# A fused two-layer block on Trainium2: the order of work in its last stage is rearranged, and some copies move to other engines and to DMA

## The chip, the cores and the metric

The program runs on one core of one Trainium2 chip. The metric is device time in microseconds (us) for one execution, as the median of several runs. One further execution was recorded by the hardware profiler; all single durations come from that record.

## The reference

Sixteen sequences of 256 rows with 256 features go through four residual steps: cross-attention to a context of 77 rows, a mixture of experts, a second cross-attention with a mask and a factor per pair, and a gated linear attention with experts. Only the last step is touched. Cut to its core, it is:

```
q1, k1, v = x @ Wq * scale, x @ Wk, x @ Wv            # 8 heads of 64
q2 = x @ Wqa @ Wqb * scale                            # low-rank path
k2 = softmax(x @ Wka @ Wkb)                           # per head
gk1 = log_sigmoid(x @ Wg1a @ Wg1b + bg1) / 16         # decay of the dense path
gk2 = log_sigmoid(x @ Wg2a @ Wg2b + bg2) / 16         # decay of the routed path
e   = softmax(x @ We)                                 # 4 experts, the best one is kept
o   = gla(q1, k1, v, gk1) + sum over experts of gla(q2*e, k2*e, v, gk2*mask)
g   = x @ Wga @ Wgb
o   = o * rsqrt(mean(o*o over a head)) * norm_w * g * sigmoid(g)
x   = x + tanh(gate) * (o @ Wo)
```

Here x is normalised over its features first. `gla` is causal linear attention with a decay per feature, kept per chunk of 64 rows in the reference.

## The kernel before

The fast path does the first steps batch by batch and the last step in `stage3_fast` (L1619). There the 16 batches are cut into slots: slot p = 4b + m works on batch b and on the pair of heads m (128 of the 512 features). `for p in range(last)` at L2056 emits the slots one by one. Every operation of an engine in this stage is tied to program order, so the text of the loop is the order of each engine's queue; the engines wait for each other by semaphores. Nearly all vector, scalar and GpSimd operations are recorded under L50 (a wrapper), the matmuls under L1637 and the transposes on TensorE under L1640.

What a slot does, with the names that the profile shows as tiles:

- `masked(p - 1, 1)` (L1917): VectorE multiplies the second product of the slot before with shares and mask, from PSUM into `at1`; GpSimd adds it to `at0` (profile: `at<-at,at`).
- `keys_queries(p + 1)` (L1834): TensorE, keys and queries of the next slot into the PSUM bank `kq`.
- `decays(p + 1)` (L1842): cumulative decays by TensorE into `gq` and `gz`, then four exponentials `ee` on ScalarE.
- `products(p, 0)` and `products(p, 1)` (L1903): query-key products of the dense and the routed path into `sc`, a pair of banks of which there is only one (pool `psa`).
- `masked(p, 0)`: VectorE, mask of the first product.
- `factors(p + 1)` and `factors_second(p + 1)` (L1888, L1895): VectorE and GpSimd multiply keys and queries with the exponentials, tiles `f`, `q`, `k`.
- `second(p + 1)` (L1854): low-rank queries into `gq`, low-rank keys of a batch ahead into `gz`.
- `summed(p)` (L2051): `values(p - 1)`, matmuls of `at` with `v` into the bank `o`, and on even p the squares of the result on ScalarE.

Around this, tables name the steps for a batch that run once in four slots. Each entry is a step, how many batches ahead it works, and perhaps an index; `run` looks up slot p % 4. They are `start` (ahead of `masked`), `copies` (behind it), `middle` (behind `keys_queries`), `rest` (ahead of `decays`), `late` (behind it), `behind_mask`, `by_rows` (behind `factors`) and `logs` (behind `factors_second`, ahead of `products(p, 1)`):

```
start = {2: [(turn_hot, 1)]}
copies = {2: [(turned_hot, 1)]}
middle = {0: [(lows, 1)], 1: [(all_gates, 1)], 2: [(pairs, 1)], 3: [(scaled, 0, 0)]}
rest = {0: [(bias, 2)], 1: [(route, 1)], 2: [(steepest, 1, 0), (stats, 2)], 3: [(steepest, 1, 1), (turn_ahead, 2)]}
late = {1: [(scaled, -1, 1)], 2: [(project, -1)], 3: [(vals, 1)]}
logs = {0: [(route_sums, 1), (outgates_end, 0, 0)], 1: [(outgates_end, 0, 1), (gate_logs, 1, 0)], 2: [(gate_logs, 1, 1), (norm_ahead, 2)]}
```

The steps: `stats`, `norm_ahead` and `turn_ahead` take the mean and variance of a batch's rows (VectorE, then four small operations on GpSimd, `rs`), normalise (ScalarE, `xn`) and transpose (`xnT`) two batches ahead. `lows` (L1689) makes the low-rank rows `low`, with the copy `lowd` by DMA and the copy `low2` on VectorE. `route_logits`, `route_sums` and `route` choose the expert (tiles `e`, `eden`, `eq`, `hot`); `turn_hot`, `turned_hot` and `pairs` turn the choice into masks (`em`, `am`). `all_gates` (L1754) makes the decays' logits in two banks and in the pair of banks `sc`. `outgates` (L1807) makes the output gate: matmuls `zg`, exponential `eg`, copy `zs`; `outgates_end` ends it with `gw` on GpSimd. `shares` and `shares_end` give the softmax's sums. `gated`, `scaled` and `project` finish a batch (`u`, `r`, `oT`, `proj`). Single banks of PSUM come from a pool of two in rotation (`pss`), others (`kq`, `gq`, `gz`, `o`) exist once.

All along, `check` collects maxima and sums; at the end `Verdict` looks at them, and if a bound was passed the program runs a slower path. `check["second"]` holds the largest sums of the second softmax.

Of the kernel before, what the change touches and what calls it, by code (L numbers as in the profile page):

```python
# [10 lines left out]
F32 = mybir.dt.float32  # L11
I32 = mybir.dt.int32
AF = mybir.ActivationFunctionType
ALU = mybir.AluOpType
AX = mybir.AxisListType
PSUM = bass.MemoryType.PSUM

P = 128
B, S, D = 16, 256, 256
# [4 lines left out]
V_LN1G, V_LN1B, V_LN2G, V_LN2B, V_QB, V_KB, V_NW, V_ONE, V_GATE, V_N = 0, 2, 4, 6, 8, 10, 12, 13, 14, 18  # L24
# [49 lines left out]
def layers(ctx: ExitStack, tc: tile.TileContext, t, out, check):  # L74
    nc = tc.nc
# [6 lines left out]
    def const(name, shape, dtype=F32):  # L82
        return cp.tile(list(shape), dtype, tag=name, name=name)


    xs, cs = [None] * B, [None] * B
# [42 lines left out]
    vec = const("vec", [P, V_N])  # L129
# [47 lines left out]
    dve3, act3, pool3 = free = [Pinned(tc, x, False) for x in (nc.vector, nc.scalar, nc.gpsimd)]  # L177
# [41 lines left out]
    def normed(dst, src, mv, rs, p=P, n=2):  # L219
        for i in range(n):  # L220
            act.activation(dst[:, i, :], src[:, i, :], AF.Identity, bias=rs[:p, 1, i:i + 1],
                           scale=rs[:p, 0, i:i + 1])

    def turned_squares(xT, x, portion):

        for n in portion:
            q, r = n // 4 * 32, n % 4 * 32
            dve.transpose(xT[r:r + 32].rearrange("p k (i s) -> p i k s", i=2)[:, :, :, q:q + 32],
                          x[q:q + 32].rearrange("p i (k d) -> p i k d", k=2)[:, :, :, r:r + 32])
# [319 lines left out]
    if fast:  # L549
        route = Route()  # L550
# [1068 lines left out]
    def stage3_fast(early_bank):  # L1619

        with ExitStack() as sx:
# [3 lines left out]
            def of(b):  # L1625

                return w1 if b % 2 else w0

            def bank(name):
                return pss.tile([P, 512], F32, tag="ps", name=name) if pss else early_bank(name)  # L1630
# [5 lines left out]
            def matmul(*a, **k):  # L1636
                tc.keep_in_program_order(nc.tensor.matmul(*a, **k))  # L1637
# [10 lines left out]
            low2 = w1.tile([64, P], F32, tag="low2", name="low2")  # L1648
# [4 lines left out]
            xn, xnT, low, lg, hT, em, am, lowd = {}, {}, {}, {}, {}, {}, {}, {}  # L1653
            v, gw, u_, oT = {}, {}, {}, {}


            mvs = {}
# [13 lines left out]

            def norm_ahead(b):
                xn[b] = w0.tile([P, 2, D], F32, tag="xn", name="xn")
                normed(xn[b], xs[b], *mvs.pop(b))

            def turn(b):
                xnT[b] = of(b).tile([P, 2, S], F32, tag="xnT", name="xnT")
# [6 lines left out]
            def turn_ahead(b):  # L1684

                xnT[b] = of(b).tile([P, 2, S], F32, tag="xnT", name="xnT")
                turned_squares(xnT[b], xn[b], range(16))

            def lows(b):  # L1689

                low[b] = of(b).tile([P, 2, S], F32, tag="low", name="low")
                ps = bank("low")
                for c in range(2):
                    for k in range(2):
                        matmul(ps[:, c * S:(c + 1) * S], la[:, k, c * P:(c + 1) * P], xnT[b][:, k, :],
                                         start=k == 0, stop=k == 1)
                dve3.tensor_copy(low[b][:, 0, :], ps[:, :S])
                dve3.tensor_scalar(low[b][:, 1, :], ps[:, S:], vec[:, V_ONE:V_ONE + 1], None, ALU.add)
                lowd[b] = of(b).tile([P, S], F32, tag="lowd", name="lowd")
                nc.sync.dma_start(out=lowd[b][64:], in_=low[b][:64, 1, :])  # L1700
                if b > 0:
                    for r in range(0, 64, 32):
                        dve3.tensor_scalar(low2[r:r + 32, :], ps[64 + r:96 + r, S + P:],
                                           vec[64 + r:96 + r, V_ONE:V_ONE + 1], None, ALU.add)

            e_, den_, z_ = {}, {}, {}

# [99 lines left out]
            def outgates(b):  # L1807

                gw[b] = w2.tile([P, 4, S], F32, tag="gw", name="gw")
                two = [bank("zg"), bank("zg")]  # L1810
                for i in range(2):
                    for h, (w, x) in enumerate(((lbg[0:64], low[b][0:64, 1, :]), (lbg2[64:], lowd[b][64:]))):
                        m = 2 * i + h
                        matmul(two[h][:, i * S:(i + 1) * S], w[:, m * P:(m + 1) * P], x, start=True, stop=True)
                for h, ps in enumerate(two):
                    e, zs = (w2.tile([P, 512], F32, tag=n, name=n) for n in ("eg", "zs"))
                    act3.activation(e, ps, AF.Exp, scale=-1.0)
                    act3.copy(zs, ps)
                    z_[b, h] = zs, e

            def outgates_end(b, h):
# [55 lines left out]
            def shares_end(b):  # L1877
                ps = z_.pop((b, "den"))
                den = w2.tile([P, 8, 32], F32, tag="dens", name="dens")
                dve3.transpose(den.rearrange("p x j -> p (x j)"), ps[:, :S])  # L1880
                rd[b] = st.tile([P, 8, 2], F32, tag="kden", name="kden")
                flat = rd[b].rearrange("p x j -> p (x j)")
                most = check["second"].rearrange("p (x j) -> p x j", j=2)
                dve3.tensor_tensor(most, most, den[:, :, 0::16], ALU.max)
                dve3.reciprocal(rd[b], den[:, :, 0::16])
                pool3.tensor_tensor(check["rsum"][:, :16], check["rsum"][:, :16], flat, ALU.add)

# [62 lines left out]
            def squares(b, mp):  # L1950
                if mp == 0:
                    u_[b] = w2.tile([P, 4, S], F32, tag="u", name="u")
                    oT[b] = w2.tile([P, 4, S], F32, tag="oT", name="oT")
                ps = o.pop((b, mp))
                sq[b, mp] = w2.tile([P, 512], F32, tag="sq", name="sq")
                act3.activation(sq[b, mp], ps, AF.Square)
                z_[b, mp, "o"] = ps
# [45 lines left out]
                    matmul(ps, ones, v[B - 1][:, 0, :], start=True, stop=True)  # L2003


            start = {2: [(turn_hot, 1)]}
            copies = {2: [(turned_hot, 1)]}
            middle = {0: [(lows, 1)], 1: [(all_gates, 1)], 2: [(pairs, 1)], 3: [(scaled, 0, 0)]}

            rest = {0: [(bias, 2)], 1: [(route, 1)], 2: [(steepest, 1, 0), (stats, 2)], 3: [(steepest, 1, 1), (turn_ahead, 2)]}  # L2010
            late = {1: [(scaled, -1, 1)], 2: [(project, -1)], 3: [(vals, 1)]}
            behind_mask = {0: [(route_logits, 1)]}
            by_rows = {0: [(outgates, 0)], 1: [(gates_end, 1)]}
            logs = {0: [(route_sums, 1), (outgates_end, 0, 0)], 1: [(outgates_end, 0, 1), (gate_logs, 1, 0)], 2: [(gate_logs, 1, 1), (norm_ahead, 2)]}

            def run(steps, p):
                for f, d, *a in steps.get(p % 4, ()):
                    if 0 <= p // 4 + d < B:
                        f(p // 4 + d, *a)
# [16 lines left out]
            w1 = sx.enter_context(tc.tile_pool(name="f3w1", bufs=1, reuse_waits="tile"))  # L2036
            w2 = sx.enter_context(tc.tile_pool(name="f3w2", bufs=2, reuse_waits="tile"))
            psa = sx.enter_context(tc.tile_pool(name="f3psa", bufs=1, space=PSUM, reuse_waits="tile"))
            pss = sx.enter_context(tc.tile_pool(name="f3ps", bufs=2, space=PSUM, reuse_waits="tile"))
            last = 4 * B  # L2040
            decays(0)
            for m in range(0, 3, 2):
                ps = bank("k2")
# [7 lines left out]
            def summed(p):  # L2051
                values(p - 1)
                if p % 2 == 0:
                    squares((p - 1) // 4, (p - 1) % 4 // 2)

            for p in range(last):  # L2056
                if p == 0:
                    turn(1)
                run(start, p)
                if p % 4 == 0:  # L2060
                    shares(p // 4)
                if 0 < p:
                    masked(p - 1, 1)
                run(copies, p)
                if p % 4 == 0:
                    shares_end(p // 4)
                if 1 < p and p % 2 == 1:
                    gated((p - 2) // 4, (p - 2) % 4 // 2)
                if p + 1 < last:
                    keys_queries(p + 1)  # L2070
                run(middle, p)
                run(rest, p)
                if p + 1 < last:
                    decays(p + 1)
                run(late, p)
                products(p, 0)
                masked(p, 0)
                run(behind_mask, p)
                if p + 1 < last:
                    factors(p + 1)  # L2080
                run(by_rows, p)

                inside = p % 4 > 0 and p + 1 < last
                if inside:
                    summed(p)
                if p + 1 < last:
                    second(p + 1)
                    factors_second(p + 1)
                run(logs, p)
                products(p, 1)  # L2090
                if 0 < p and not inside:
                    summed(p)

            b, p = B - 1, last - 1
# [126 lines left out]
```

## Time and profile before

| what | value |
|---|---|
| median of 3 runs | 1845.09 us (1840.51 to 1845.21) |
| profiled execution, its own time | 1847.08 us |
| span of the profiled execution | 1845.3 us |
| last stage, one batch in its steady part | 37.72 us |
| TensorE busy over the span | 1813.5 us (98%) |
| VectorE, ScalarE, GpSimd busy | 1231.5, 873.9, 1017.0 us |
| granted TensorE clock, mean | 0.995 |

The span runs from the first to the last instruction of the program in the profiled execution. The names in a row are the tile written, an arrow, and the tiles read; then the shapes, the number of instructions and, in brackets, the idle time before and what ended it. PE stands for TensorE, PEld for its weight loads, DVE for VectorE, ACT for ScalarE, POOL for GpSimd and SPq for the queue that issues DMAs. A matmul's end is modelled in such a record, so distances between starts are the better measure of TensorE's pace. A row in a timeline that holds several instructions gives the time from the first start to the last end.

### The profile page before, as it was taken

Reading aid. Unit: us, or ns where it says so; the run is one execution under the profiler, and the core shown is the slowest. Engines: PE = TensorE matmul, PEld = TensorE weight load, DVE = VectorE, ACT = ScalarE, POOL = GpSimd, SP = SyncE. Lnnn points to the kernel's source line nnn. Section 1 sums busy time; section 2 is a strip of 40 time slices with the busy share of each in tenths; the row PEclk is TensorE's granted clock in tenths of the full one; section 3 lists DMA queues with packets and bytes.
Section 4 is the critical chain, followed back from the end, with each engine's and each line's share of the span. In section 5 each row is a group of like instructions: output and inputs, shape, how many; then the busy total and the mean of one; then the engine's idle time right before and its main releaser. Section 6 shows DMA issues by size and latency. Waiting matters only on the chain.

```text
span 1845.3 us, 35182 instructions
## 1 busy us (share of the span) xinstructions
PE 1813.5 (98%) x13870; PEld 1249.8 (68%) x13870; DVE 1231.5 (67%) x2903; ACT 873.9 (47%) x1804; POOL 1017.0 (55%) x1001
## 2 busy tenths in 40 slices
PE   8999999999999999999999999999999999999997
PEld 5666666666766667666777766656767777777765
DVE  3355656566665666656474488867888878878874
ACT  4433344433444334443433487846555645455543
POOL 4654767567676576756634767315444444444433
PEclk9999999999999999999999999999999999999999
DMA  9800010000010100000077933100000000000000
GB/s 304 226 1 22 16 34 15 25 17 23 23 37 8 29 19 10 31 23 18 13 248 238 233 49 49 18 4 3 14 8 10 8 10 13 8 9 8 14 9 14
DMA packets 68504, 85.86 MB, mean 47 GB/s; under 512 B 10740, under 2 KB 55908, under 8 KB 67818
## 3 DMA queue, kind: packets, MB, share of 16 engines
q1 hardware_dynamic: 56041, 66.74, 11.5%
q0 software_dynamic: 12288, 16.79, 4.5%
q8 instruction: 111, 1.82, 0.4%
q14 instruction: 64, 0.52, 0.1%
HBM read 44.17 MB, written 38.29 MB: 45 GB/s over the span
## 4 chain that ended last, share of the span: by engine, by line
PE 82%; POOL 9%; DVE 4%; issue 2%; ACT 2%; DMA 1%; SPq 0%; POOLq 0%; DVEq 0%; ACTq 0%
PE o L50 11%; PE qk L50 11%; PE v L50 8%; PE sc L50 8%; PE proj L50 7%; PE kq L1637 7%; PE sc L1637 5%; POOL es L50 4%; PE gq L1637 3%; PE v L1637 3%; PE o L1637 3%; PE proj L1637 3%; POOL x L50 2%; PE ex L50 2%; POOL rs L50 2%
## 5 line engine op out<-in xcount | busy, mean ns | idle before, releaser
L50 POOL TENSOR_SCALAR rs<-mv 128x2 f32<-128x2 f32 (+2 forms) x85 | 16.3, 192 | 376.8 <-DVE mv L50 371.1
L50 DVE RECIPROCAL rd<-o 128x256 f32<-128x256 f32 x64 | 112.3, 1755 | 164.0 <-PE o L50 123.7
L50 POOL TENSOR_TENSOR at<-at,at 128x768 f32<-128x768 f32 x63 | 114.1, 1812 | 142.4 <-DVE at L50 142.4
L50 ACT ACTIVATE e<-sc 128x1024 f32<-128x1024 f32 (+1 forms) x192 | 181.7, 1016 | 18.4 <-PE sc L50 18.4
L50 PE MATMUL sc<-qk 64*128 64x256 f32 (+1 forms) x1536 | 183.1, 384 | 0.5 <-DVE qk L50 0.5
L50 PE MATMUL o<-e,v 128*32 128x256 f32 (+1 forms) x3072 | 177.9, 379 | 0.0
L50 PEld LDWEIGHTS sc<-qk 64*128 64x128 f32 (+1 forms) x1536 | 132.0, 172 | 55.1 <-issue 26.8
L50 POOL TENSOR_TENSOR esum<-esum,es 128x512 f32<-128x512 f32 x128 | 163.5, 1277 | 10.0
L50 PE MATMUL qk<-kvT,wkv 128*128 128x333 f32 x512 | 164.3, 443 | 0.0
L50 ACT ACTIVATE qk<-qk 128x256 f32<-128x256 f32 x128 | 48.8, 381 | 231.4 <-PE qk L50 231.4
L50 POOL TENSOR_TENSOR es<-e 128x1024 f32<-128x1024 f32 x64 | 151.2, 2363 | 12.1 <-ACT e L50 9.0
L50 POOL TENSOR_TENSOR es<-es,e 77x1024 f32<-77x1024 f32 x64 | 150.4, 2350 | 5.0
L50 PEld LDWEIGHTS o<-e,v 128*32 128x32 f32 (+1 forms) x3072 | 99.9, 110 | 66.3
L50 PE MATMUL qk<-kvT,wq 128*128 128x256 f32 x512 | 134.6, 385 | 0.0
L50 DVE COPY qk<-qk 128x333 f32<-128x333 f32 x128 | 64.6, 504 | 93.8 <-ACT qk L50 92.8
L50 POOL DMA_INDIRECT x<-rows_out,pos x64 | 101.1, 1580 | 33.2 <-issue 17.0
L50 PEld LDWEIGHTS qk<-kvT,wq 128*128 128x128 f32 x512 | 94.3, 189 | 35.2 <-issue 9.6
L50 PEld LDWEIGHTS qk<-kvT,wkv 128*128 128x128 f32 x512 | 97.2, 190 | 30.0
L50 PE MATMUL proj<-wo0h,oT 128*128 128x256 f32 x512 | 113.7, 380 | 0.3 <-DVE oT L50 0.3
L50 PE MATMUL v<-wkv,kvT 128*128 128x512 f32 x256 | 113.1, 595 | 0.0
L50 PEld LDWEIGHTS proj<-wo0h,oT 128*128 128x128 f32 x512 | 95.9, 190 | 13.9 <-issue 0.8
L50 POOL DMA_INDIRECT rows<-xw,pos x64 | 66.8, 1043 | 61.1 <-ACT xT L50 24.0
(265 smaller groups left out, 4085.7 us busy)
## 6 DMA issues: line engine op xcount, KB each, us to landing
rows<-zero SPq DMA_DIRECT2D x16, 640.0 KB
xin<-rows SPq DMA_DIRECT2D x16, 640.0 KB
rows_out<-y SPq DMA_DIRECT2D x16, 384.0 KB
v<-vctx SPq DMA_DIRECT2D x15, 308.0 KB
x<-in_x_dram SPq DMA_DIRECT2D x16, 256.0 KB
rows_out<-y SPq DMA_DIRECT2D x16, 256.0 KB
out_dram<-x SPq DMA_DIRECT2D x15, 256.0 KB
wkv<-in_wkv_dram SPq DMA_DIRECT2D x2, 1024.0 KB
```

What stands on the lines that cost most here:

```text
L50: x = getattr(self.engine, name)(*a, **k)
L1637: tc.keep_in_program_order(nc.tensor.matmul(*a, **k))
```

## The change

It touches `stage3_fast` alone, in these parts:

- `turn_ahead`: instead of 16 transposes of blocks on VectorE, one operation transposes every 32x32 square in place into a new tile `turned`, and 16 DMAs on the SP queue bring the squares to their places in `xnT`. `norm_ahead` writes its rows in another order of squares for that.
- `lows`: `low2` is copied by a DMA from `low` instead of by two VectorE operations from PSUM.
- `outgates`: the copies `zs` are made by VectorE instead of ScalarE.
- `shares_end`: the maximum of a batch goes into a column of its own by one reduction, instead of a running maximum of two tiles.
- `squares`: `oT` uses `u`'s tile.
- The tables: `turn_hot` moves behind `keys_queries` of slot 2, `pairs` to the start of slot 3, `route` and `stats` behind the factors of slot 1, `norm_ahead` to slot 2 ahead of `decays`, `turn_ahead` to the end of slot 2, `steepest` to slot 3 for both halves. `copies` is gone.
- `inside`: the values of the slot before also go ahead of `second` in the first slot of a batch, where they stood behind `products(p, 1)`.

```diff
             def norm_ahead(b):
                 xn[b] = w0.tile([P, 2, D], F32, tag="xn", name="xn")
-                normed(xn[b], xs[b], *mvs.pop(b))
+                every = "p i (k d) -> p i k d"
+                normed(xn[b].rearrange("p k (i d) -> p i k d", i=2), xs[b].rearrange(every, k=2), *mvs.pop(b))
...
                 xnT[b] = of(b).tile([P, 2, S], F32, tag="xnT", name="xnT")
-                turned_squares(xnT[b], xn[b], range(16))
+                y = w1.tile([P, 4, P], F32, tag="turned", name="turned")
+                dve3.transpose(y.rearrange("p x d -> p (x d)"), xn[b].rearrange("p k d -> p (k d)"))
+                to = xnT[b].rearrange("p k (i s) -> p (k i) s", i=2)
+                for q in range(0, P, 32):
+                    for r in range(0, P, 32):
+                        nc.sync.dma_start(out=to[r:r + 32, :, q:q + 32], in_=y[q:q + 32, :, r:r + 32])
...
                 if b > 0:
-                    for r in range(0, 64, 32):
-                        dve3.tensor_scalar(low2[r:r + 32, :], ps[64 + r:96 + r, S + P:],
-                                           vec[64 + r:96 + r, V_ONE:V_ONE + 1], None, ALU.add)
+                    nc.sync.dma_start(out=low2, in_=low[b][64:, 1, P:])
...
                     act3.activation(e, ps, AF.Exp, scale=-1.0)
-                    act3.copy(zs, ps)
+                    dve3.tensor_copy(zs, ps)
...
-                most = check["second"].rearrange("p (x j) -> p x j", j=2)
-                dve3.tensor_tensor(most, most, den[:, :, 0::16], ALU.max)
+                dve3.tensor_reduce(check["second"][:, b:b + 1], den[:, :, 0::16], AX.XY, ALU.max)
...
-                    oT[b] = w2.tile([P, 4, S], F32, tag="oT", name="oT")
+                    oT[b] = u_[b]
...
-            start = {2: [(turn_hot, 1)]}
-            copies = {2: [(turned_hot, 1)]}
-            middle = {0: [(lows, 1)], 1: [(all_gates, 1)], 2: [(pairs, 1)], 3: [(scaled, 0, 0)]}
-
-            rest = {0: [(bias, 2)], 1: [(route, 1)], 2: [(steepest, 1, 0), (stats, 2)], 3: [(steepest, 1, 1), (turn_ahead, 2)]}
+            start = {3: [(pairs, 1)]}
+            middle = {0: [(lows, 1)], 1: [(all_gates, 1)], 2: [(turn_hot, 1)], 3: [(scaled, 0, 0)]}
+
+            rest = {0: [(bias, 2)], 2: [(turned_hot, 1), (norm_ahead, 2)], 3: [(steepest, 1, 0), (steepest, 1, 1)]}
...
-            logs = {0: [(route_sums, 1), (outgates_end, 0, 0)], 1: [(outgates_end, 0, 1), (gate_logs, 1, 0)], 2: [(gate_logs, 1, 1), (norm_ahead, 2)]}
+            logs = {0: [(route_sums, 1), (outgates_end, 0, 0)],
+                    1: [(route, 1), (stats, 2), (outgates_end, 0, 1), (gate_logs, 1, 0)],
+                    2: [(gate_logs, 1, 1), (turn_ahead, 2)]}
...
-                inside = p % 4 > 0 and p + 1 < last
+                inside = 0 < p and p + 1 < last
```

More of the change, by code (lines that the diff above doesn't have):

```diff
@@ L2063, in stage3_fast @@
                     masked(p - 1, 1)
-                run(copies, p)
                 if p % 4 == 0:
```

## The prediction

> **What bounds the kernel now.** First the page's engine row and its slices, then the window table for one batch of the last stage, then the timelines of that batch engine by engine (13th of 0 to 15, four slots, 37.72 us; its neighbours take 37.72 and 37.70).
>
> ```profile
> PE 1813.5 (98%) x13870; PEld 1249.8 (68%) x13870; DVE 1231.5 (67%) x2903; ACT 873.9 (47%) x1804; POOL 1017.0 (55%) x1001
> ...
> 1721.96:1759.68 37.72, 37.52 (x246) 27.12 (x245) 30.75 (x75) 20.22 (x46) 17.78 (x18) 1.00 0.03 10
> ```
>
> TensorE is busy for 37.52 of 37.72 us; no other engine is near that. The change takes no matmul away and adds none. So all it can win is time in which TensorE stands still, and all it can lose is a new wait in TensorE's queue. The real stops are read from distances between starts, as ends are modelled. TensorE's timeline where slot 0 goes over into slot 1:
>
> ```profile
> 1728.79 0.38 PE L1637 MATMUL gq<-low,lbk 64*128 64x256 f32 x1
> ...
> 1729.13 0.38 PE L1637 MATMUL gz<-low,lbk 64*128 64x256 f32 x1
> 1729.69 0.92 PE L1637 MATMUL sc<-q,k 64*128 64x256 f32 x8 [0.19 <-DVE e L50]
> 1730.54 0.87 PE L1637 MATMUL o<-at,v 128*64 128x256 f32 x8
> 1731.34 1.13 PE L1637 MATMUL kq<-xnT,wk 128*128 128x256 f32 x4
> ...
> 1733.27 0.70 PE L1637 MATMUL z<-lbg,low 17*128 17x512 f32 x2
> 1733.28 0.70 PE L1637 MATMUL sc<-lbg,low 17*128 17x512 f32 x2
> ```
>
> These matmuls follow each other at some 0.11 us, so after 1729.13 the next could start at 1729.24; it starts at 1729.69, when VectorE has read the routing rows (`e`) out of the shared `sc` bank. That 0.45 us, once a batch, is nearly all the idle time there is to win. (A second stop, 0.18 us ahead of `products` while `low` is copied, is not touched.)
>
> VectorE in the same batch, then GpSimd and the DMA queue:
>
> ```profile
> 1729.46 0.68 DVE L50 TENSOR_TENSOR f<-kq,ee 128x512 f32<-128x512 f32 x1
> 1730.06 0.41 DVE L50 TENSOR_TENSOR q<-gq,ee 128x256 f32<-128x256 f32 x1
> ...
> 1730.66 1.39 DVE L50 SCALAR_TENSOR_TENSOR at<-sc,kden,am 128x256 f32<-128x256 f32 x4
> ...
> 1734.79 1.54 DVE L50 TENSOR_TENSOR eq<-e,em 128x8 f32<-128x8 f32 x1
> 1736.37 0.17 DVE L50 TENSOR_TENSOR eq<-eq,prio 128x8 f32<-128x8 f32 x1
> ```
>
> ```profile
> 1734.49 1.82 POOL L50 TENSOR_TENSOR at<-at,at 128x768 f32<-128x768 f32 x1
> 1738.44 1.28 POOL L50 TENSOR_TENSOR oT<-u,r 128x512 f32<-128x512 f32 x1 [2.14 <-ACT r L50]
> 1739.68 0.73 POOL L50 TENSOR_TENSOR k<-e,ee 128x256 f32<-128x256 f32 x1
> ```
>
> ```profile
> 1727.17 0.47 SPq L1700 DMA_DIRECT2D lowd<-low  x1
> ```
>
> Two things to see: the four `at` operations of slot 1 end at 1732.05, 1.2 us before `all_gates` (the `z` and `sc` rows at 1733.27) needs the `sc` bank that they read; and a tiny `eq` takes 1.54 us, ending with GpSimd's `at` (1736.31).
>
> **The change, part by part**, in us per batch, against 37.72.
>
> *A, values inside slot 0.* The `o` matmuls go ahead of `second` and the late `sc`. Now `zg` to `kq` is 1727.92 to 1731.34, 3.42. After: zg 0.87, o 0.80, second 0.54, sc 0.75 (steps of slot 1: 1737.14, 1737.94, 1738.48, 1739.23), 2.96, and up to 0.1 for changing from 64 to 128 rows; I take 3.01. The wait for `e` (done 1729.55) is covered. **-0.41**, 15 batches (batch 0 has no earlier values there): -6.2.
>
> *B, the zs copies go from ScalarE to VectorE.* ScalarE wasn't the bound; nothing is won there. On VectorE they stand between `f` and `q`, so ahead of slot 1's `at`. No row has a 128x512 copy from PSUM. Below: `low`'s 128x256 copy starts 0.34 before its follower; above: `f`, 128x512 with two inputs, 0.60 between starts. Same length as `f`, so 0.60 each, 1.20 the pair. `at` then begins at 1731.86 and ends at 1733.25; with 0.07 to be noticed, 1733.32. `all_gates` would come at 1733.27 - 0.41 = 1732.86, as its four matmuls start together. It waits **+0.46**: what A won is given back three steps later. 14 batches, and 0.86 in batch 0, where TensorE comes 0.8 earlier: +7.3. With 0.34 copies it would be nothing.
>
> *C, choice behind the factors.* `route` moves from slot 1's start to its end, `turn_hot` from slot 2's start to behind `keys_queries`. VectorE is free for `route` after `q` at about 1739.18 (1738.80 + 0.33 + the 0.05 that A and B leave). Its seven operations take 0.2 each where nothing holds them (1736.37 to 1737.13 for four). The question is the 1.54 of `eq`. Row: its mean is 1.37. [...] So what counts is GpSimd at the new place: `oT` to 1739.7, then `k` to 1740.45. First product behind `oT`, 1739.8; `eq` behind `k`, 1740.48; four more, hot done at 1741.28, noticed 1741.34. TensorE asks at 1738.53 + 0.75 + 1.87 = 1741.15. Wait **+0.2**, 15 times: +3.0. By the mean of the row alone, hot would be done at 1742.0 and the wait 0.9, +13.5; if nothing blocked, zero. That `hT` and `both` change neighbours costs 0 (bounds ±0.1: the first matmul of a new kind comes 0.1 later or not, in either order).
>
> *D, statistics behind the choice.* Their 0.96 of VectorE follows `route`, to 1742.3; GpSimd's four `rs` operations (1.53, from 1745.20 to 1746.73 now) wait for that, and queued behind them are slot 1's `gw` (1.23) and the addition of `at` (1.81): 1742.37, 1743.90, 1745.13, 1746.94. The `o` matmuls of slot 2 want that sum; with `both` gone from slot 2, TensorE gets there at 1741.34 + 0.25 + 0.95 + 3.5 + 0.85 = 1746.9. **+0.1**, 14 times (no statistics for the last two batches): +1.4; 0 to 0.3. `norm_ahead` on ScalarE holds up four `ee`, to 1747.3; `f` needs them at 1747.9.
>
> *E, rows turned by DMA.* 16 block transposes (5.03 of VectorE, hidden under `vals`) become one of 128x512 (about 0.7 from `dens`, 0.44 for 256) and 16 DMAs on SP. Nothing won: VectorE's 5 us were covered by TensorE's 1752 to 1757. Cost: SP starts at about 1749.6. An issue takes 0.47 (`lowd`, also SBUF to SBUF), 0.46 to 0.48 between starts where SP issues in a row at 926 to 929; I take 0.52. `lowd`'s bytes are through 1.57 after its issue began (its DMA window: 1727.17 to 1728.74). 15 x 0.52 + 1.57 = 9.4, landed at 1759.0; `lows` wants them at about 1762.5. Hidden, with 3.5 to spare; the point is a pace of 0.75. [...] these runs are 128. One DMA has 128 of them, 8 per engine; a `lowd` packet of 1024 bytes takes some 0.07, so 8 are under 0.6 even at that price: at worst a pace of 0.6, 10.6 in all. Same answer. What remains: `lows` waits for the completion semaphores of many DMAs[...]. Before shows no such case; a single awaited semaphore is taken up within 0.14 (`e` done 1729.55, `sc` 1729.69). From 0 (looked at while `kq` runs) to 0.5; I take **+0.2**, nearer to one pick-up than to many: 14 times, +2.8.
>
> *F, the rest.* low2 by DMA: landed near 1729.5, wanted at 1733. `second` as a reduction: 1.3 of VectorE saved where VectorE then waits for `low` anyway (idle 0.72). `oT` in `u`'s place, `steepest` in slot 3 where the transposes were: 0; TensorE's four us of `vals` cover them.
>
> **Sum:** -6.2 + 7.3 + 3.0 + 1.4 + 2.8 = +8.3. The profiled execution's span of 1845.3 becomes 1853.6 (its own time 1847.1, 2.0 above the median of the runs, becomes 1855.4); the runs' median of 1845.1 becomes **1853**.
>
> **Rivals.** *The copies are cheap* (not slower): if the pair takes at most 0.74 on VectorE, B vanishes; 1853 - 7.3 = 1846. For it: a copy has one input. Against it: `low`'s and `hT`'s copies take 0.40 to 0.42 for 256, no less per element than `f`. *The DMAs are late* (slower still): above a pace of 0.75 each 0.1 costs 1.5 a batch; at 0.85, 1853 + 14 x 1.5 = 1874. For it: issues 0.75 apart stand at the program's start, with large loads in flight. Against it: the DMA share is 0.03 here. *Waits fold* (no change): D and E's pick-ups vanish behind C's wait and B is 0.3; 1853 - 1.4 - 2.8 - 2.2 = 1847. For it: each late point leaves the next engine time to catch up. *A alone* (faster): every late point is hidden by slack that I don't see; 1845.1 - 6.2 = 1839. Against it: B's chain is made of operations back to back.
>
> **How the numbers follow.** About 0.3% (5.5 us) can be told from no change. My sum 0.60, folding 0.20, cheap copies 0.08, late DMAs 0.07, A alone 0.05. Of the sum's own range (1848 to 1861: C from 0 to 0.5, pick-ups 0 to 0.4) about a twentieth of the chance lies within 5.5 of now; with folding and cheap copies that makes same 0.32. Slower is the rest of the sum and the late DMAs, 0.63; faster 0.05. Range 1843 to 1865.
>
> **What would show it.** A right: the `e` wait gone and `o` ahead of the late `sc`. B right: TensorE's `sc<-lbg,low` waits for VectorE's `at`, some 0.4 a batch. C right: `hT` waits for `hot`; `eq` ends with GpSimd's `k`. D: `o` waits for GpSimd's `at`. E: `low<-xnT` starts without a long DMA wait. A batch then takes 38.2 to 38.4. I am wrong if it takes 37.3 (no new waits), or if `low` waits for DMAs by more than 0.5.

## The result

The changed kernel takes **1851.12 us** (median of 6 runs, 1849.61 to 1853.36), the kernel before 1844.49 (6 runs beside it, 1840.51 to 1846.48): a ratio of 1.0044, 95% interval 1.0034 to 1.0054. The forecast of 1853 was 1.9 us too high. Its parts fit far less well than its sum (a steady batch was to take 38.2 to 38.4 us), and that is what the experiments are about.

The profiled execution of the changed kernel took 1853.36 us, with a span of 1851.6 us at a mean granted clock of 0.995. The engine row of its page, and the window of one steady batch (columns as in the window before: stretch, length, busy time with instructions of PE, PEld, DVE, ACT and POOL, granted clock, DMA share, GB/s):

```profile
PE 1819.1 (98%) x13870; PEld 1253.7 (68%) x13870; DVE 1143.2 (62%) x2695; ACT 860.5 (46%) x1772; POOL 1015.7 (55%) x1001
...
1727.88:1765.72 37.84, 37.82 (x249) 27.39 (x245) 24.34 (x61) 19.40 (x44) 17.73 (x18) 1.00 0.08 17
```

VectorE lost 88 us of work over the span and 6.4 us per batch, and nothing came of it: TensorE was the bound and is the bound. Its number of matmuls is the same, and a batch takes 37.84 us instead of 37.72.

TensorE's timeline of the changed kernel, slot 0 into slots 1 and 2 of the 13th batch:

```profile
1734.04 0.38 PE L1637 MATMUL zg<-lowd,lbg 64*128 64x256 f32 x1
1734.34 0.87 PE L1637 MATMUL o<-at,v 128*64 128x256 f32 x8
...
1735.68 0.82 PE L1637 MATMUL sc<-q,k 64*128 64x256 f32 x8
1736.43 1.13 PE L1637 MATMUL kq<-xnT,wk 128*128 128x256 f32 x4
1737.40 1.03 PE L1637 MATMUL kq<-xnT,wq 128*128 128x256 f32 x4
1738.35 0.70 PE L1637 MATMUL z<-lbg,low 17*128 17x512 f32 x2
1738.88 0.70 PE L1637 MATMUL sc<-lbg,low 17*128 17x512 f32 x2
1738.89 0.59 PE L1637 MATMUL z<-lbg,low 17*128 17x512 f32 x2
1739.41 0.59 PE L1637 MATMUL sc<-lbg,low 17*128 17x512 f32 x2
1739.93 0.71 PE L1637 MATMUL gq<-dmask,lg 128*128 128x128 f32 x4
...
1746.65 0.38 PE L1640 MATMUL hT<-ident,hot 128*4 128x128 f32 x2
1746.87 0.61 PE L1637 MATMUL gq<-dmask,lg 128*128 128x128 f32 x4
...
1751.32 0.92 PE L1637 MATMUL sc<-f 64*128 64x256 f32 x8
1752.17 0.87 PE L1637 MATMUL o<-at,v 128*64 128x256 f32 x8
```

The values now stand ahead of the late `sc`, and the stop of 0.45 us for `e` is gone. In its place the `sc` rows of `all_gates` start 0.53 us behind `z` (1738.35, 1738.88), where both started together before. `hT` follows `kq` without a gap, and `o` follows `sc` at the usual 0.85.

VectorE in the same stretch, then GpSimd:

```profile
1735.65 1.29 DVE L50 COPY zs<-zg 128x512 f32<-128x512 f32 x2 [0.17 <-ACT eg L50]
1736.85 0.41 DVE L50 TENSOR_TENSOR q<-gq,ee 128x256 f32<-128x256 f32 x1
...
1737.45 1.37 DVE L50 SCALAR_TENSOR_TENSOR at<-sc,kden,am 128x256 f32<-128x256 f32 x4
...
1745.12 0.45 DVE L50 TENSOR_TENSOR eq<-e,em 128x8 f32<-128x8 f32 x1
1745.60 0.17 DVE L50 TENSOR_TENSOR eq<-eq,prio 128x8 f32<-128x8 f32 x1
...
1746.20 0.17 DVE L50 TENSOR_TENSOR hot<-eq,e 128x8 f32<-128x8 f32 x1
```

```profile
1744.81 0.73 POOL L50 TENSOR_TENSOR k<-e,ee 128x256 f32<-128x256 f32 x1
1747.34 0.19 POOL L50 TENSOR_SCALAR rs<-mv 128x2 f32<-128x2 f32 x1 [1.79 <-DVE mv L50]
...
1750.09 1.81 POOL L50 TENSOR_TENSOR at<-at,at 128x768 f32<-128x768 f32 x1
```

The four `at` end at 1738.82, and the `sc` rows start 0.06 later: that is the wait. The pair of copies before them began only when ScalarE's `eg` had read the first bank (the bracket), which the prediction did not have. `eq` is held by GpSimd's `k` until 1745.54, yet the choice is ready at 1746.37, 0.28 us before TensorE asks.

Among TensorE's waits in the last stage (L1637 and L1640) only three lines are missing or smaller in the kernel before (us in total, times, longest):

```profile
PE o L1637 <- POOL at L50: 2.4, 1, 2.4
...
PE hT L1640 <- DVE hot L50: 0.8, 1, 0.8
...
PE low L1637 <- issue: 0.2, 1, 0.2
```

All three are single events. The first is in the first batch, the second in the last but one; in the third, rows turned by DMA land late for the last batch. The 0.53 us of every batch is in no line, since `z`, waiting for nothing, overlaps it in the record; only the distance between starts shows it.

### The profile page after: what moved, and what is told of

It reads as the page before. It is cut to its first block, busy times and chain, and to the rows that moved or that the text cites. A ratio compares the mean times of both kernels' runs of the same rounds, so it can differ in the third digit from the quotient of the medians.

```text
span 1851.6 us, 35290 instructions
## 1 busy us (share of the span) xinstructions
PE 1819.1 (98%) x13870; PEld 1253.7 (68%) x13870; DVE 1143.2 (62%) x2695; ACT 860.5 (46%) x1772; POOL 1015.7 (55%) x1001
## 4 chain that ended last, share of the span: by engine, by line
PE 85%; POOL 7%; DVE 4%; issue 1%; ACT 1%; DMA 1%; POOLq 0%; SPq 0%; DVEq 0%; ACTq 0%
PE o L50 11%; PE qk L50 11%; PE v L50 9%; PE sc L50 8%; PE proj L50 7%; PE kq L1637 7%; PE sc L1637 6%; PE gq L1637 4%; POOL es L50 4%; PE v L1637 3%; PE proj L1637 3%; PE o L1637 3%; PE ex L50 3%; POOL rs L50 2%; PE gz L1637 2%; PE low L1637 2%
## 5 line engine op out<-in xcount | busy, mean ns | idle before, releaser
L50 DVE TENSOR_TENSOR at<-sc,amask 128x768 f32<-128x768 f32 x64 | 61.3, 957 | 124.5 <-PE sc L1637 124.5
```

The lines of the kernel that those rows point to most:

```text
L50: x = getattr(self.engine, name)(*a, **k)
```

## The experiments

The measure for most of them is the distance between the starts of `kq` in successive slots of a steady batch (number 6 of 0 to 15; the others agree within 0.03 us, but for the first two, the last two and those for which the rows turned by DMA land late, told of under E). A column is named after the slot in which the stretch begins; slot 3 is that of the batch before.

| kernel | slot 3 | slot 0 | slot 1 | slot 2 | batch | ratio to before, 95% interval |
|---|---|---|---|---|---|---|
| before | 10.66 | 8.81 | 8.10 | 10.15 | 37.72 | |
| changed | 10.62 | 8.56 | 8.39 | 10.27 | 37.84 | 1.0044 (1.0034 to 1.0054) |
| e3, before + values inside | 10.65 | 8.55 | 8.10 | 10.15 | 37.46 | 0.9985 (0.9976 to 0.9993) |
| e2, before + zs on VectorE | 10.65 | 8.81 | 8.36 | 10.15 | 37.97 | 1.0017 (1.0010 to 1.0024) |
| e4, before + both | 10.65 | 8.55 | 8.61 | 10.15 | 37.97 | 1.0014 (1.0008 to 1.0021) |
| e1, changed, zs on ScalarE | 10.62 | 8.55 | 7.88 | 10.59 | 37.64 | 1.0034 (1.0020 to 1.0047) |
| e5, changed, half of zs on ScalarE | 10.62 | 8.55 | 8.77 | 10.28 | 38.22 | 1.0073 (1.0054 to 1.0092) |
| e7, changed, gw ahead of statistics | 10.62 | 8.55 | 8.39 | 11.21 | 38.78 | 1.0103 (1.0086 to 1.0120) |
| e6, changed, rows turned early | 10.62 | 8.55 | 8.40 | 10.28 | 37.84 | 1.0035 (1.0021 to 1.0048) |
| e8, e1 + choice turned late | 10.62 | 8.55 | 7.88 | 10.50 | 37.55 | 1.0017 (1.0006 to 1.0029) |
| b3, e8 + three more edits | 10.62 | 8.47 | 7.88 | 10.51 | 37.48 | 1.0023 (1.0013 to 1.0033) |
| b1, before + values ahead of zg | 10.65 | 8.55 | 8.10 | 10.15 | 37.45 | 0.9980 (0.9973 to 0.9986) |
| b2, b1 + low's half first | 10.66 | 8.46 | 8.10 | 10.15 | 37.38 | 0.9985 (0.9975 to 0.9995) |
| b4, before + inside but for the end + low's half first | 10.65 | 8.50 | 8.10 | 10.15 | 37.41 | **0.9974** (0.9961 to 0.9987) |

One caution on the last column. The mean granted clock differs between runs, and the span with it: in a straight line fitted to the 135 runs of the kernel before, by 1.5 us for each 0.001. The dips in the clock lie mostly around the start of the last stage. The runs of e1, e8 and b3 had mean clocks of 0.9937, 0.9952 and 0.9936, those of before 0.9965. So for these three the ratios mix the batch with the clock, and the distances decide about the waits.

### A: values inside slot 0, alone (e3)

```diff
-                inside = p % 4 > 0 and p + 1 < last
+                inside = 0 < p and p + 1 < last
```

> The kernel before with the values ahead of second in slot 0 too and nothing else. Theory: the wait for e goes, o behind zg costs 0.2 more than I had summed; -0.26 a batch, batch 37.46, -3.9 us in 15 batches, ratio 0.998. Rival (the wait only moves to the next slot): ratio 1.000.

Measured: median 1840.6, ratio 0.9985, 37.46 us a batch. A gives 0.26 us in slot 0 and disturbs nothing behind it in the steady part. It does so 14 times, not 15: the last batch has no choice to prepare, so nothing waited for `e` there, as the kernel before shows:

```profile
PE sc L1637 <- DVE e L50: 2.6, 14, 0.2
```

The difference to the 0.41 of the prediction sits in one place: the first `o` starts 0.30 us behind the last `zg` (1734.04 to 1734.34 above), where these matmuls otherwise come some 0.11 apart. The last batch's last slots lost 0.39 us (24.23 instead of 23.84 from the last batch's first `kq` on).

### B: the zs copies, alone and with A (e2, e4)

```diff
-                    act3.copy(zs, ps)
+                    dve3.tensor_copy(zs, ps)
```

> The kernel before with the zs copies on VectorE and nothing else. Theory: at of slot 1 ends at 1733.25 where the sc banks are wanted at 1733.27; the 1.2 us of slack are just used up, ratio 0.999 to 1.001, batch 37.70 to 37.80. Rival (each copy costs VectorE time that ends up in the total): +0.5 a batch, +7 us, ratio 1.004.

Measured: 37.97 us a batch, ratio 1.0017, so 0.25 us lost where none was expected. VectorE's copies in this kernel:

```profile
1462.79 1.29 DVE L50 COPY zs<-zg 128x512 f32<-128x512 f32 x2 [0.16 <-ACT eg L50]
```

The copies do not start when VectorE is free, but 0.16 us later, when ScalarE's `eg` has read the bank, and the pair takes 1.29 instead of the 1.20 counted on. The two make up the 0.25; the expectation had neither.

> The kernel before with both: values ahead of second in slot 0, zs copies on VectorE. Theory: the two do not add; -0.26 from the first, then +0.5 of waiting at all_gates: +0.25 a batch, batch 37.95, +3.5 us, ratio 1.002. Rival (they add): e2 plus e3, about -3.9 us, ratio 0.998.

Measured: 37.97, ratio 1.0014, as expected. A's 0.26 and B's +0.25 don't add to nothing by themselves: with A, slot 0 is 0.26 shorter and slot 1 is 0.51 longer than before. What A wins, B takes back, because the copies hold `at` to the same time whether TensorE comes early or late.

### B undone in the changed kernel (e1)

```diff
-                    dve3.tensor_copy(zs, ps)
+                    act3.copy(zs, ps)
```

> The changed kernel with the two zs copies on ScalarE again. Theory (a wait for the sc banks): VectorE's at of slot 1 ends 1.2 us sooner, all_gates no longer waits 0.53 a batch, batch 37.84 becomes about 37.3; 14 batches give -7.5 us, so about 1843.6, slightly below the kernel before (ratio 0.999). Rival (the time goes to the many small DMAs and the batch 0 and 14 waits, the copies only use idle time): 1850 to 1851, ratio about 1.004.

Measured: 1852.51, ratio 1.0034; the clock (above) leaves the total undecided. The batch does decide: slot 1 drops by 0.51 us to 7.88, so B's wait is real. But slot 2 grows by 0.31, and a batch is only 0.20 us shorter. VectorE and GpSimd of this kernel in slot 1, then TensorE's answer:

```profile
1479.96 0.61 DVE L50 TENSOR_TENSOR e<-e,eden 128x8 f32<-128x8 f32 x1
...
1480.80 0.46 DVE L50 TENSOR_TENSOR eq<-e,em 128x8 f32<-128x8 f32 x1
...
1481.89 0.17 DVE L50 TENSOR_TENSOR hot<-eq,e 128x8 f32<-128x8 f32 x1
```

```profile
1479.27 1.27 POOL L50 TENSOR_TENSOR u<-u,r 128x512 f32<-128x512 f32 x1 [1.40 <-ACT r L50]
1480.51 0.72 POOL L50 TENSOR_TENSOR k<-e,ee 128x256 f32<-128x256 f32 x1
```

```profile
1482.20 0.38 PE L1640 MATMUL hT<-ident,hot 128*4 128x128 f32 x2 [0.15 <-DVE hot L50]
```

The first operation of `route` ends with GpSimd's `u` (1480.57 and 1480.54), the first `eq` with its `k` (1481.26 and 1481.23), as step C had it. TensorE's `kq` of this slot starts at 1480.05, 0.5 us earlier against GpSimd than in the changed kernel: `k` ends 1.18 us behind the start of `kq` here, 0.72 there. So the wait of C exists; in the changed kernel the wait of B hides it.

### Half of the copies (e5)

```diff
-                    dve3.tensor_copy(zs, ps)
+                    (dve3.tensor_copy if h else act3.copy)(zs, ps)
```

> The changed kernel with the second half of zs (h = 1) on VectorE and the first half back on ScalarE. The theory: VectorE's copy of a half cannot start before ScalarE's reading of the same half (eg) has ended, so a copy on VectorE is late by what ScalarE does ahead of it. With the first half back, ScalarE does eg 0, zs 0 and eg 1 one after the other, VectorE's copy starts about 1 us after where it starts now for the first half and no earlier than now for the second; the end of the copies stays at or behind today's. The first piece of all_gates then waits between 0.5 (today) and 0.9 us, slot 1 lasts 8.5 to 8.9, a batch 37.8 to 38.2 us: no gain over the changed kernel's 37.84. The rival (the wait comes of VectorE's having two copies to do): with one copy instead of two the wait falls to nothing or to a quarter microsecond, and a batch lasts 37.3 to 37.6 us.

Measured: 38.22 us a batch, ratio 1.0073. The wait of `all_gates` is 0.90 us instead of 0.53, with half the copying. VectorE and TensorE of this kernel:

```profile
1743.95 0.69 DVE L50 COPY zs<-zg 128x512 f32<-128x512 f32 x1 [1.14 <-ACT eg L50]
```

```profile
1745.68 1.13 PE L1637 MATMUL z<-lbg,low 17*128 17x512 f32 x4
1746.58 1.13 PE L1637 MATMUL sc<-lbg,low 17*128 17x512 f32 x4
```

VectorE stood 1.14 us for ScalarE's second `eg`, which ran 1743.30 to 1743.91 behind `eg`, `zs` on ScalarE. The rival is out: the amount that VectorE copies does not set the price of B alone. With half of it, the later start costs more than the 0.60 us of copying saved, as `q` and `at` stand behind the copy and wait with it for the other reader of its bank.

### C: the choice turned later, with zs on ScalarE (e8)

```diff
-            middle = {0: [(lows, 1)], 1: [(all_gates, 1)], 2: [(turn_hot, 1)], 3: [(scaled, 0, 0)]}
+            middle = {0: [(lows, 1)], 1: [(all_gates, 1)], 3: [(scaled, 0, 0)]}
...
-            rest = {0: [(bias, 2)], 2: [(turned_hot, 1), (norm_ahead, 2)], 3: [(steepest, 1, 0), (steepest, 1, 1)]}
-            late = {1: [(scaled, -1, 1)], 2: [(project, -1)], 3: [(vals, 1)]}
+            rest = {0: [(bias, 2)], 2: [(norm_ahead, 2)], 3: [(steepest, 1, 0), (steepest, 1, 1)]}
+            late = {1: [(scaled, -1, 1)], 2: [(turn_hot, 1), (turned_hot, 1), (project, -1)], 3: [(vals, 1)]}
```

> The changed kernel with both halves of zs on ScalarE, and the choice's transposition (turn_hot, turned_hot) issued by TensorE behind slot 2's decays, ahead of project, instead of behind its logits. With zs on ScalarE alone a batch lasted 37.64 us (10.62, 8.55, 7.88, 10.58), and there hT waited 0.3 us more than in the changed kernel. The theory: that wait is all that slot 2 and 3 lost, and behind the decays the choice has long been made: a batch lasts 37.33 us, 0.39 less than before the change, 14 times 0.39 = 5.5 us less over the stage, of which batch 0's wait of o for the statistics (2.4 us) and the late rows of single batches (about 1.6) are given back: about 1843, ratio 0.998 to 1.000. The rival (another wait takes the place of hT's, as the decays' own inputs come from ScalarE too): a batch stays at 37.6, 1847 or more, ratio 1.001 to 1.003.

Measured: 1847.39, ratio 1.0017, 37.55 to 37.57 us a batch. The theory said 37.33; the rival was right, though not by way of the decays' inputs. `hT` waits no more in the steady batches, and most of the gain is gone at the next `o`:

```profile
1491.69 0.92 PE L1637 MATMUL sc<-f 64*128 64x256 f32 x8
1492.77 0.87 PE L1637 MATMUL o<-at,v 128*64 128x256 f32 x8 [0.15 <-POOL at L50]
```

```profile
1488.15 0.19 POOL L50 TENSOR_SCALAR rs<-mv 128x2 f32<-128x2 f32 x1 [1.79 <-DVE mv L50]
...
1489.67 1.27 POOL L50 TENSOR_TENSOR gw<-zs,eg 128x512 f32<-128x512 f32 x1
1490.90 1.81 POOL L50 TENSOR_TENSOR at<-at,at 128x768 f32<-128x768 f32 x1
```

```profile
PE o L1637 <- POOL at L50: 2.2, 13, 0.2
```

The last fence is from TensorE's waits in the steady part. `o` comes 1.08 us behind `sc` instead of 0.85. This is step D as predicted: the four `rs` of the statistics push `gw`, and `gw` pushes the addition that `o` wants. With the wait of C in front of it, D cost nothing; without it, D costs 0.23.

### D: gw ahead of the statistics (e7)

```diff
-                    1: [(route, 1), (stats, 2), (outgates_end, 0, 1), (gate_logs, 1, 0)],
+                    1: [(route, 1), (outgates_end, 0, 1), (stats, 2), (gate_logs, 1, 0)],
```

> The changed kernel with slot 1's outgates_end ahead of the statistics, so that GpSimd makes gw while VectorE is in route. Theory [...]: the second eq takes about 1.2 instead of 0.17 as in batch 14 of the changed kernel, hT waits for hot by about 0.8 in every batch, batch 38.6, +10 us against the changed kernel, ratio 1.010; the 2.4 us wait of o in batch 0 gets shorter by up to 1.2. Rival (the chain of statistics, gw and addition on GpSimd is what costs): faster than the changed kernel, by the 2.4 us of batch 0.

Measured: 1861.15, ratio 1.0103, 38.78 us a batch, as expected. TensorE's waits:

```profile
PE hT L1640 <- DVE hot L50: 10.9, 14, 0.8
...
PE o L1637 <- POOL at L50: 1.5, 1, 1.5
```

With `gw` ahead of the statistics, the choice is late by 0.8 us for TensorE in 14 batches. The statistics, which stood between, had kept GpSimd waiting for `mv` (1.79 us ahead of `rs` in the changed kernel) and so had kept `gw` away from `route`. In the last but one batch of the changed kernel, which has no statistics, `eq` stands until `gw` ends without any edit. VectorE and GpSimd there:

```profile
1784.20 1.25 DVE L50 TENSOR_TENSOR eq<-eq,ec 128x8 f32<-128x8 f32 x1
```

```profile
1784.16 1.26 POOL L50 TENSOR_TENSOR gw<-zs,eg 128x512 f32<-128x512 f32 x1 [0.42 <-ACT eg L50]
```

An operation on 8 elements takes 1.25 us instead of 0.17 and ends at 1785.45, 0.03 behind `gw`. What the first batch waits for `at` fell from 2.4 to 1.5, so by 0.9, less than the 1.26 that `gw` takes.

### E: the rows turned earlier (e6)

```diff
-            behind_mask = {0: [(route_logits, 1)]}
+            behind_mask = {0: [(route_logits, 1)], 2: [(turn_ahead, 2)]}
...
-                    2: [(gate_logs, 1, 1), (turn_ahead, 2)]}
+                    2: [(gate_logs, 1, 1)]}
```

> The changed kernel with turn_ahead right behind the first mask of slot 2 instead of at the slot's end. The 16 DMAs then start about 0.9 us sooner. Theory (in the batches where one issue takes 1.3 to 1.7 us instead of 0.6, the last landing is later than lows, which waits 0.1 to 0.4): those waits vanish, all batches take 37.8 to 37.9, -1.6 us against the changed kernel, ratio to the kernel before about 1.003. Rival (lows does not wait for DMAs, those batches differ for another reason): the same uneven batches, ratio 1.0044.

Measured: 1851.6, ratio 1.0035. The total can't be told from that of the changed kernel. In the trace all the batches from the third to the fourteenth take 37.84 us, where five of the changed kernel's take 37.94 to 38.30, and the last but one takes 38.77 instead of 39.14: from the third batch's start to the last's 492.8 us against 494.5. The late rows are gone, and they had been worth 1.6 us in all. The changed kernel's transfers of that kind for one batch, on the queue:

```profile
1754.95 11.45 SPq L1693 DMA_DIRECT2D xnT<-turned  x16
```

Sixteen issues take 10.33 us in a calm batch, 0.60 each and 0.65 apart (the prediction: 0.52), and 11.0 to 11.5 in the later batches, where one issue takes 1.3 to 1.7 us. The long ones stay in e6 (up to 1.67), but land in time.

### Building on A (b1, b2, b4) and on the changed kernel (b3)

b1 runs `outgates` behind the values in slot 0; b2 adds the second half of `low` written ahead of the first. The core of both:

```diff
-                run(by_rows, p)
+                if p % 4:
+                    run(by_rows, p)
...
+                if p % 4 == 0:
+                    run(by_rows, p)
```

> The kernel before with the values of slot 0 ahead of second and also ahead of zg. Theory: the 0.2 that o lost behind zg is won back, as zg runs straight into second; batch 37.3, -0.42 in 15 batches, -6.3 us, ratio 0.9966. Rival (the eviction of zg, now 0.8 later, holds up all_gates' banks): 37.46 or more, ratio 0.9985 or above.

Measured: 1840.63, 37.45 us. Nothing over e3: slot 0 lasts 8.55 us in both, so the 0.2 does not come back in this order, and the last slots lose 0.9.

> The same, and in lows the half of low that the routing transposes wait for is written first. Theory: the stop of 0.18 us ahead of products in slot 0 goes too, batch 37.12, another -2.7 us, about 1835, ratio 0.995. Rival (the transposes then wait for the semaphore of the pair of writes as before): as b1.

Measured: 1841.13, 37.38 us. 0.08 of the 0.18 expected.

b4 keeps the order of before in the last batch and writes low's half first:

```diff
-                inside = p % 4 > 0 and p + 1 < last
+                inside = 0 < p < last - 4 or p % 4 > 0 and p + 1 < last
...
-                dve3.tensor_copy(low[b][:, 0, :], ps[:, :S])
                 dve3.tensor_scalar(low[b][:, 1, :], ps[:, S:], vec[:, V_ONE:V_ONE + 1], None, ALU.add)
+                dve3.tensor_copy(low[b][:, 0, :], ps[:, :S])
```

> The kernel before with two edits only: values inside slot 0 as well, but for the last batch, which keeps its order; and the second half of low written ahead of the first. Values inside alone gave 37.46 us a batch with 0.4 us lost in the last slot; low's half first gave 0.09 on top of another order. The theory: 37.37 us a batch, 14 times 0.35 = 4.9 us less than the kernel before and nothing lost at the end: about 1839.5, ratio 0.997. The rival (low's half first pays only with values ahead of the z products): 37.46, ratio 0.998 to 0.9985.

Measured: 1839.70 (before beside it 1844.65), ratio 0.9974, 37.41 us a batch, and 23.84 us at the end as before. Low's half first pays 0.05 here, between theory and rival; with the end undisturbed this has the lowest ratio of all, some 5 us under the kernel before, though its interval overlaps b1's and b2's.

b3 adds to e8 three edits: the rows turned behind slot 2's mask, low's half first, and the first batch's statistics back in slot 2. The last of them:

```diff
-            rest = {0: [(bias, 2)], 2: [(norm_ahead, 2)], 3: [(steepest, 1, 0), (steepest, 1, 1)]}
+            rest = {0: [(bias, 2)], 2: [(stats, 2), (norm_ahead, 2)], 3: [(steepest, 1, 0), (steepest, 1, 1)]}
...
-                    if 0 <= p // 4 + d < B:
+                    if 0 <= p // 4 + d < B and not (f is stats and (p == 1 if steps is logs else p > 2)):
```

> The kernel of the run before this one (zs on ScalarE, the choice turned behind slot 2's decays) with three more edits: the rows' transfers issued behind slot 2's mask rather than at its end, the second half of low written ahead of the first, and the statistics of the first batch ahead of slot 2 again. The theory: 37.33 less 0.09 for low = 37.24 us a batch, no late rows, and no wait of 2.4 us in batch 0: 14 times 0.48 = 6.7 us less than the kernel before, 1837 to 1839, ratio 0.996 to 0.997. The rival (rows by DMA keep a price of their own in the last batches, or the order with the choice late costs what it saves): 1842 or more, ratio over 0.998.

Measured: 1848.69, ratio 1.0023, 37.48 us a batch: a miss. In the steady batches `o` still waits for `at` as in e8, 0.24 us that the expectation did not hold. In the first batch the 2.4 us did not vanish but moved: `o` waits 0.5 instead of 2.44, and the low-rank queries wait 2.4 for ScalarE's `ee`, which stands behind `xn`, which waits for the same `rs`. TensorE's waits and ScalarE's row in this kernel:

```profile
PE gq L1637 <- ACT ee L50: 2.4, 1, 2.4
```

```profile
1258.58 1.09 ACT L50 ACTIVATE xn<-x,rs 128x256 f32<-128x256 f32 x2 [4.08 <-POOL rs L50]
```

The steady 0.24 and these 2.4 explain 14 x 0.24 + 2.4 = 5.8 us over the 1837 to 1839 expected; of the some 5 us that are left, the mean clock of 0.9936 against 0.9965 would make some 4.4, an estimate at 1.5 us for each 0.001. In five of the six kernels whose profile has a stop of 2.4 us in the first batch (e1, e5, e6, e8, b3) the granted clock falls near its end; in the changed kernel it does not, nor in e7, where the stop is 1.5, nor in before and b4, which have none. Windows of e8 (the granted clock is the third figure from the end), around `o` at 1262.96, which waited 2.44, then windows of the changed kernel, around `o` at 1259.01, which waited as long:

```profile
1258.62:1262.03 3.41, 1.58 (x14) 1.02 (x13) 2.62 (x7) 2.09 (x6) 3.24 (x5) 1.00 0.01 2
1262.03:1272.27 10.24, 9.31 (x33) 6.91 (x34) 5.03 (x11) 2.01 (x4) 3.01 (x3) 0.50 0.07 11
1272.27:1275.68 3.41, 3.41 (x15) 1.97 (x15) 1.32 (x2) 2.44 (x7) 1.31 (x2) 1.00 0.16 26
```

```profile
1254.39:1257.80 3.41, 1.87 (x17) 1.44 (x15) 2.62 (x7) 1.80 (x6) 3.15 (x6) 1.00 0.01 2
1257.80:1261.21 3.41, 2.20 (x21) 1.68 (x22) 1.15 (x3) 1.60 (x5) 1.84 (x2) 1.00 0.00 0
1261.21:1264.62 3.41, 3.41 (x14) 2.55 (x15) 3.02 (x8) 0.70 (x1) 0.31 (x1) 1.00 0.09 14
```

At 0.50 the 10.24 us lack 5.1 us of work at full clock, of which up to 0.5 falls into the stop itself. The edges of the dips lie on a grid of 3.41 us in each profile (in before they begin at 1056.22, 1213.24 and 1824.22, 46 and 179 steps apart), and every dip that is not cut off by the program's end lasts one, two or three such steps. Laid over that grid, the stops differ: in e1, e5, e6, e8 and b3 one step holds 1.8 to 2.5 us in which TensorE stands (e8: 3.41 - 1.58 = 1.83), and the clock falls with the next; in the changed kernel the stop is split into 1.54 and 1.21, and in e7 no step has more than 1.53. In these five, then, a step of 3.41 with 1.8 us or more without work was followed by a fall; that the stop is its cause is not shown, as no run made for it has tried it. Nor is the time that TensorE stands the whole measure: around the start of the stage dips follow steps with only 0.5 to 1.2 us of it. The clocks over all runs speak for a part only: 0.9937, 0.9952 and 0.9936 for e1, e8 and b3, but 0.9962, 0.9961 and 0.9963 for the changed kernel, e6 and e5, with the same stop.

## Why the prediction was right, and where it was not

The sum was +8.3 us; the medians say +6.6, the two profiled spans +6.3. Summed from the trace of the changed kernel against that of before:

| step | predicted | found | where it shows |
|---|---|---|---|
| A | -6.2 | -3.6 | e3: 0.26 x 14 |
| B | +7.3 | +7.4 | 0.51 x 14 in slot 1; e1, e4; 0.29 in the first batch |
| C | +3.0 | +0.9 | 0 in steady batches, the last but one +0.93 |
| D | +1.4 | +2.4 | 0 in steady batches, the stop in the first 2.44 |
| E | +2.8 | +1.6 | no pick-ups; late rows in six batches |
| order of `hT`, `both`, masks | 0 | -1.8 | 0.13 x 14 (-0.22, +0.12 and -0.03 in slots 1, 2 and 3) |
| last slots of the last batch | 0 | +0.3 | as in e3 |
| behind the last `kq` | 0 | -1.0 | one more step at half clock in before |
| sum | +8.3 | +6.2 | |

Each line is good to some tenths. The order's line is what is left of a steady batch, 0.12, after A and B (37.84 - 37.72 + 0.26 - 0.51 = -0.13). Up to the end of the first batch both records have lost the same to the clock, three steps of 3.41 us at half.

That 1853 came so near is luck in good part. The sum made a steady batch 0.5 to 0.7 us longer, and it is 0.12 longer, 1.7 us in 14 batches. The rest of what was lost lies in events that stand outside the steady part or come in some batches only (2.44 in the first, 0.93 in the last but one, 1.6 in late rows), and the prediction had none of these.

**What bounds the kernel** held: VectorE's 88 us less gave nothing.

**A** had the right mechanism and the wrong size. The failing term is "up to 0.1 for changing from 64 to 128 rows": between `zg` and `o` it is 0.30, of which 0.11 is the normal step. Why it is more than at other such changes (0.20 from the last `sc` to `o` in slot 0 of before) is open. And it wins 14 times, not 15.

**B** held, place and size (0.46 predicted, 0.51 to 0.53 found), but the size by errors that partly cancel. The step "they stand between `f` and `q`" left out that each copy follows ScalarE's `eg` on its bank: VectorE stood idle for 0.17 us until `eg` ended in the changed kernel, for 1.14 in e5. The trace of before has no such wait, as `eg` and `zs` are both ScalarE's there. So `at` is late by 0.17 of waiting and by 0.09 of copying (1.29 for the pair instead of 1.20) that were not counted; and as A brings TensorE only 0.26 earlier instead of 0.41, `all_gates` comes 0.15 later than counted. e2 (loss without A) and e5 (more loss with half the copies) show the missing term. The 0.86 of the first batch was 0.29 (slot 1 lasts 8.18 there, 7.89 in e1). The rival of cheap copies fell because the pair took 1.29, where it needed 0.74 or less.

**C** failed in its steady size. "Wait +0.2, 15 times" assumed that GpSimd's `oT` and `k` keep their distance to TensorE. They come earlier against it (`k` ends 0.72 behind the start of `kq` instead of e1's 1.18), because ScalarE and GpSimd run on while TensorE stands in B's wait. e1, without that wait, has C's 0.31. That an operation of `route` ends with the GpSimd operation beside it, as in before (`eq` at 1736.33, `at` at 1736.31), was seen again: `eq` ended with `k` (1745.57 and 1745.54; 1481.26 and 1481.23 in e1), in e1 `e` ended with `u` (1480.57 and 1480.54), in the last but one batch `eq` ended with `gw` (1785.45 and 1785.42), each within 0.03 us. Why it does is not shown. By the row's mean C would have cost 13.5. What the step missed is that with no statistics in the queue `gw` comes early and hits `route`, +0.93 once.

**D** failed in the same way, "+0.1, 14 times" being 0 behind the waits ahead of it and 0.23 without them (e8). And it missed the first batch, where no projection of an earlier batch gives TensorE 3.5 us of work to cover the chain: 2.44 at once.

**E**'s pick-ups, "+0.2, 14 times", an estimate for which before had no case, don't exist: in a calm batch `low` starts 1.83 us behind `kq`, as before. The pace was 0.65, over the 0.52 taken and below the 0.75 at which it was said to matter. The worst case drawn from a `lowd` packet, 0.6, was close, but for another reason: the queue's row shows that the issues themselves, 0.60 each with 0.05 between them, set the pace. Of the 3.5 us to spare little was left. In calm batches the last bytes arrive 11.2 us behind the first issue instead of 9.4, 1.0 to 1.4 ahead of `low`; where `low` waits, it starts 0.4 to 0.8 behind them. One issue of 1.3 to 1.7 was then too much, and six batches, none of them in the first half, lost 0.1 to 0.46 each.

The rival **waits fold** (1847) was the better picture of the mechanism, though what folded was C behind B, and it had B at 0.3. Its number was farther off, because it did not have the single events either. The chance given to the sum was too high for how it is made: three late points in a row of one queue were added, and e1 and e8 show that each hides the next.

## What to carry to other kernels

Late points along one in-order queue did not add here: the first wait gives the other engines time to catch up, and when it is removed the next comes forth (B, then C, then D, 0.51 giving back 0.31, and 0.31 giving back 0.23). So cost them as a chain, and test a repair by the distance of the whole loop, not by the wait that it removes. Before a copy goes to another engine, ask which engine reads the same bank before it (the copy stood 0.17 us for that reader in the changed kernel, 1.14 in e5), and what stands behind the copy in its new queue; and look at the first and the last turns of the loop apart, where what covers a chain in the steady part is missing.

## What was not expected of the hardware

- From the last `zg` matmul (64 rows) to the first `o` (128 rows) 0.30 us pass, three steps instead of one; from the last `sc` (64 rows) to `o` in slot 0 of before it is 0.20.
- An issue of the SBUF-to-SBUF transfer with 128 runs of 128 bytes took 0.60 us against `lowd`'s 0.47 to 0.51, and one in sixteen took 1.3 to 1.7 in the later batches. In the trace of the changed kernel a transfer of instructions begins in the issue just ahead of each of the seven long ones, but other such transfers are followed by none; that they are the cause was not tried.
- The granted clock falls to 0.50 in dips of 3.41, 6.83 or 10.24 us at different places, mostly around the start of the last stage; three of the fourteen profiles (e2, e7, b2) have none ahead of the program's end. In e8 such a dip of 10.24 us began in a stop of 2.44 us; in the changed kernel a stop as long was followed by none. Runs of one kernel differ by some 1.5 us of span for 0.001 of mean clock.
